# Eight placing transfers instead of twelve, and unit-first step order in the first eighth of every phase

## The chip, the cores and the metric

The kernel runs on one core of a Trainium2 chip. The metric is device time in microseconds (us). A core has five instruction streams that run side by side and meet through semaphores: TensorE (PE, with its weight loads PEld), VectorE (DVE), ScalarE (ACT), GpSimd (POOL) and SyncE (SP), which here only issues transfers (DMAs). Each stream is in order: an instruction that waits holds up all that stand behind it.

## The reference, cut to what matters

Four residual layers act on images `(4, 32, 32, 16)`. Three are of one kind, and they make up nearly all the work; layer 2 is another, small computation on intervals. For a layer of the first kind, with `n` the group-normalised input:

```python
first  = einsum('ijyx,byxc->bijc', M, n)
kern   = transpose(G, (0, 1, 5, 4, 2, 3)).reshape(h * w * f, c, 3, 3)
shifted = conv(n, kern, 'SAME')          # a 3x3 convolution with 1024*16 filters
diff   = relu(n[:, None, None] - shifted)
second = einsum('ijyx,bijyxc->bijc', W, diff)
x      = x + first - second
```

For each of the 1024 places (i, j), each filter f and each image b there is a whole 32x32 picture, which is clipped, weighted with `W` and summed to one number.

## The kernel before, in words

The four images go in two groups `g` of two (`GB` = 2). A phase is one group in one of the three convolution layers, six in all, in the order layer 0 group 0, layer 0 group 1, layer 1 group 0, and so on. The 1024 places are eight blocks `t` of 128 (`NT` = 8). In a block there are 32 steps, one for each filter f and image b. So a phase has 256 steps, and the program 1536. They are all issued by `conv_layer` (L707).

One step makes a 128x1024 picture in a pair of PSUM banks (there are four such pairs): `first_part` (L642) issues eight matmuls on `ib` and `ia`, ACT scales the pair in place (L663), and `second_part` (L666) adds six matmuls on `iyz` and `im9`. Then one DVE instruction (L680, tile `junk`) takes the minimum with zero, multiplies by the chunk of `W` (tile `WT`) and adds up. Step k's second part is issued after step k+1's first part.

The matmuls reach more than the precision of one pass by splitting both operands into a high and a low part. Weights: `prep_parts` (L220) makes, for each unit of four filters (`FU` = 4; 192 units, eight steps each), the tiles `parts` and `W9`. DVE cuts off the high part (L203, tile `upper_w`), ACT and POOL make the others (L236 to L245), POOL subtracts the centre tap from the next unit's raw weights (L214), and SP copies one half of `parts` to the other with halves swapped (L251) and loads raw weights two units ahead (L110). Its `yield`s spread these over the eight steps of a unit.

Images: before a phase, `before_conv` (L368) normalises the next group, writes it to DRAM, reads it back shifted (L392, tile `raw`), and then, for each of the two images b in turn:

- `split` (L274): DVE cuts the high part (L203, tile `upper_x`), POOL subtracts it (L280, twice, for the two slots s), and ACT scales it (L284, twice). The results are `tz` and `ty`, the two halves (index k) of one tile `temp`, laid out as (k, s, b, n) with n = 512. In the first phase the tile is `first`, and DVE takes POOL's place.
- `place` (L290): SP copies pieces of `ty` and `tz` into `ia` (L298) and `ib` (L300).
- `difference` (L286, L288): POOL (DVE in the first phase) writes `iyz`; then `halve_rest` (L178) on DVE finishes `im9`.

The generator `behind` (L733) hands these out a bit after each step, so their place in every engine's order is fixed when the program is built. For phases 1 to 3 the images are split and placed well inside the phase before; for phases 4 and 5, whose interval layer comes first, in the last eighth of it.

Each SP transfer uses one of eight completion semaphores in turn. So a transfer's issue waits until the transfer eight issues earlier has landed.

Before the change the 32 steps of a block run filter by filter, image 0 then image 1. Only in the very first block (`n == 0`) are they sorted by unit: four filters of image 0, then the same four of image 1.

Of the kernel before, what the change touches and what calls it, by code (L numbers as in the profile page):

```python
# [8 lines left out]
F32 = mybir.dt.float32  # L9
F32R = mybir.dt.float32r  # L10
# [5 lines left out]
P = 128  # L16
B, H, C = 4, 32, 16
NG = 2
GB = B // NG
# [5 lines left out]
HW = H // 2  # L25
WP = HW + 2
PITCH = H * WP
NH = H * HW
RUN = (H - 1) * WP + HW
LAST = (H - 1) * HW  # L30
TAPS = ((0, 1, 2, 3), (6, 7, 4, 5))
TEMP = 2 * 2 * GB * NH
# [12 lines left out]
def net_kernel(ctx: ExitStack, tc: tile.TileContext, x, xq, xi, convs, iv_w, iv_b, out):  # L45
# [26 lines left out]
    nc = tc.nc  # L72
# [6 lines left out]
    big = ctx.enter_context(tc.tile_pool(name="big", bufs=1))  # L79
# [32 lines left out]
    def load_chunk(n):  # L112
        if n < n_chunks:
            t = n % NT
            chunks[n] = wpool.tile([P, NP], F32, tag="WT", name=f"WT_{n}")
            nc.sync.dma_start(chunks[n], convs[phases[n // NT][1]][1][t * P : (t + 1) * P, :])
# [15 lines left out]
    first = big.tile([P, 8192], F32, tag="big", name="first")  # L132
    used = PLAIN * 3 * FU * P
# [40 lines left out]
    def halve(dst, src, mask):  # L174
        nc.scalar.activation(dst, src, AF.Copy, scale=mask[:, 1:2])  # L175

    def halve_rest(dst, src, mask):
        nc.vector.scalar_tensor_tensor(  # L178
            dst, src, mask[:, 0:1], dst.bitcast(F32), op0=ALU.mult, op1=ALU.add
        )  # L180
# [13 lines left out]
    QUARTERS = [(slice(64 * h, 64 * h + 32), slice(64 * h + 32, 64 * h + 64)) for h in range(2)]  # L194

    def image(v, x):
        return v.rearrange("... (y x) -> ... y x", x=x)[..., :HW]
# [69 lines left out]
    def prep_plain_rest(u, at=0, to=FU):  # L267
        halve_rest(units[u][3][:, at:to], raws[u][:, 2, at:to], low_p)

    def halves(temp, b):  # L270
        v = temp.rearrange("p (k s b n) -> p k s b n", k=2, s=2, b=GB)
        return v[:, 0, :, b], v[:, 1, :, b]

    def split(eng, g, b, temp, name, pause=IDLE):  # L274

        ty, tz = halves(temp, b)
        high = upper(image(raw[:, :2, b], WP), 2, f"x{name}{b}")
        yield 1
        for s in range(2):
            eng.tensor_tensor(  # L280
                image(tz[:, s], HW), image(raw[:, s, b], WP), image(high[:, s], HW), ALU.subtract
            )
            yield pause
            nc.scalar.activation(ty[:, s], high[:, s], AF.Copy, scale=EPS)  # L284

    def difference(eng, g, b, s, temp):  # L286
        ty, tz = (v.bitcast(F32)[:, s] for v in halves(temp, b))
        eng.tensor_tensor(iyz[g][:, s, b], ty, tz, ALU.subtract)  # L288

    def place(g, b, temp):  # L290

        ty, tz = (v.bitcast(F32) for v in halves(temp, b))
        da, db = (v[g].bitcast(F32)[:, :, b] for v in (ia, ib))
        for h, (lo, hi) in enumerate(QUARTERS):
            for s in range(2):
                at = HW if s == h else 0
                for to, src in ((lo, ty), (hi, tz)):
                    nc.sync.dma_start(da[to, s, :LAST], src[lo, s, at : at + LAST])  # L298
            for to, src in ((lo, ty), (hi, tz)):
                nc.sync.dma_start(db[to], src[hi])  # L300
        yield 1


# [64 lines left out]
    def before_conv(g, layer):  # L368
        xn = work.tile([P, NT, GC], F32, tag="xn", bufs=2, name=f"xn_{g}_{layer}")
        xns[g] = xn  # L370
        yield from group_norm(g, f"c{g}{layer}", xn, 1 if layer == 2 else 4)

        nc.vector.transpose(
            xt[g][:, :, 1 : 1 + H], xn
        )
        inner = xs[g][:, :, WP : WP + H * WP].rearrange("p h (t r n) -> p h r t n", r=ROWS, n=WP)
        for r in range(ROWS):
            for h in range(2):  # L380
                nc.sync.dma_start(
                    inner[:, h, r], xt[g][GC * r : GC * (r + 1), :, HW * h : HW * h + WP]
                )
        yield 2
        xsv = xs[g].rearrange("(b c) h n -> c h b n", b=GB)
        for slot, row, tap in [
            (slot, row, tap) for slot in range(2) for row, tap in enumerate(TAPS[slot])
        ] + [(2, row, 8) for row in range(4)]:
            for h in range(2):
                off = tap // 3 * WP + tap % 3  # L390
                r0 = 64 * h + C * row
                nc.sync.dma_start(  # L392
                    raw[r0 : r0 + C, slot ^ h if slot < 2 else 2, :, :RUN], xsv[:, h, :, off : off + RUN]
                )
            if layer < 2 or row % 2:
                yield 1
        yield 6 if layer == 2 else 12
        temp = big.tile([P, 8192], F32R, tag="big", name=f"temp_{g}{layer}")[:, :TEMP]
        for b in range(GB):
            yield from split(nc.gpsimd, g, b, temp, f"{g}{layer}")  # L400
            yield IDLE
            halve(image(im9[g][:, b], HW), image(raw[:, 2, b], WP), low_x)
            yield from place(g, b, temp)
            for s in range(2):
                difference(nc.gpsimd, g, b, s, temp)
            yield 1
            halve_rest(image(im9[g][:, b], HW), image(raw[:, 2, b], WP), low_x)
            yield 1
# [233 lines left out]
    def first_part(step):  # L642
        phase, t, f, b = step
        g = phases[phase][0]
        n = phase * NT + t
        u = n * NU + f // FU
        ps = bank_pair(f"pc_{n}_{f}_{b}")
        if u < PLAIN:
            products(
                ps,  # L650
                [(raws[u][:, s, f % FU], image(raw[:, s, b], WP)) for s in range(2)]
                + [(units[u][3][:, f % FU], im9[g][:, b])],
                True, {2: without_last},
            )
            return ps
        WU, WL, WD, W9 = (w[..., f % FU, :] for w in units[u])
        products(
            ps,
            [(WL[:, s], ib[g][:, s, b]) for s in range(2)]
            + [(WU[:, s], ia[g][:, s, b]) for s in range(2)],  # L660
            True, {2 + s: without_outer(s) for s in range(2)},
        )
        nc.scalar.activation(ps, ps, AF.Copy, scale=1.0 + EPS)  # L663
        return ps
# [42 lines left out]
    def conv_layer(phase, behind):  # L707


        kind, wait = 1, 0  # L710
        accs[phase] = work.tile([P, NT, GC], F32, tag="acc", bufs=2, name=f"acc_{phase}")
        for t in range(NT):
            n = phase * NT + t
            steps = [(f, b) for f in range(C) for b in range(GB)]
            if n == 0:
                steps.sort(key=lambda s: (s[0] // FU, s[1]))
            for at, (f, b) in enumerate(steps):
                may = next(parts, (IDLE, CALM)) if n or at >= FIRST else (IDLE, CALM)
                if n == 0 and at in (20, 24):
                    next(parts)  # L720
                if at == 4:
                    load_chunk(n + 1)
                step = (phase, t, f, b)
                open_steps.append((step, first_part(step)))
                if len(open_steps) > 1:
                    second_part(*open_steps.pop(0))
                wait -= 1
                if wait <= 0 and (kind > 0 or kind in may):
                    kind = wait = next(behind, 1 << 20)
        for _ in behind:  # L730
            pass
# [137 lines left out]
    def rest_of_start():  # L869

        nc.sync.dma_start(X[0], x[0])
        load_raw(2)
        load_raw(3)
        prep_plain_rest(0, F0, FU)
        for slot in (0, 1, 2):
            normal(nc.vector, 1, slot)
            sides(nc.vector, 1, slot)
        halve(image(im9[0][:, 1], HW), image(raw[:, 2, 1], WP), low_x)
        prep_plain(1)
        prep(2)  # L880
        yield 1
        halve_rest(image(im9[0][:, 1], HW), image(raw[:, 2, 1], WP), low_x)
        prep_plain_rest(1)
        yield 2
        temp = first.bitcast(F32R)[:, used : used + TEMP]
        for b in range(GB):
            yield from split(nc.vector, 0, b, temp, "00", 1)
            yield from place(0, b, temp)
            for s in range(2):
                difference(nc.vector, 0, b, s, temp)  # L890
            yield 1
        nc.gpsimd.memset(zero, 0.0)
        nc.vector.memset(part, 0.0)
        zeros(0)
        xns[0] = work.tile([P, NT, GC], F32, tag="xn", bufs=2, name="xn_00")
        yield from group_norm(0, "c00", xns[0], 4)

    parts = prep_parts()
# [81 lines left out]
```

## Time and profile before

| | us |
|---|---|
| median of three runs | 2477.86 (2477.18 to 2479.97) |
| the profiled execution | 2478.41 |
| its span, first to last instruction | 2476.7 |
| PE busy | 2458.2 |
| DVE / ACT / POOL busy | 2087.3 / 1878.4 / 1579.7 |
| L680 on DVE, mean of one | 1.224 |
| placing transfers: `ia` from `temp` x80, from `first` x16; `ib` x40 and x8 | to landing 3.4 and 2.6 (medians for `temp`) |
| raw weights (L110) x190 | to landing 7.1 |

In the rows of the profile, "out<-in" names what an instruction writes and reads, "Lnn" is the line of the program, and "<-" in a bracket names what ended the idle time before the instruction. "SPq" is SP's issue of a transfer. The granted clock of TensorE was 1.0 for the whole span.

### The profile page before, as it was taken

How to read it: one execution, taken by the hardware profiler on the slowest of the kernel's cores; microseconds unless marked ns; L12 is line 12 of the kernel's file. 1: busy time of each engine (PE TensorE's matmuls, PEld its weight loads, DVE VectorE, ACT ScalarE, POOL GpSimd, SP SyncE). 2: the span in 40 equal slices, each digit the busy share in tenths (PEclk: the TensorE clock that was granted, in tenths of full speed). 3: DMA queues.
4: the chain of work that ended last, by engine and by line, in shares of the span. 5: the costliest groups of instructions: out<-in, count | busy, mean ns of one | idle time of the engine just before them, and what ended most of it. 6: DMA issues, size and time to landing. Idle time of an engine off the chain costs nothing.

```text
span 2476.7 us, 58058 instructions
## 1 busy us (share of the span) xinstructions
PE 2458.2 (99%) x21906; PEld 2090.1 (84%) x21906; DVE 2087.3 (84%) x3617; ACT 1878.4 (76%) x2181; POOL 1579.7 (64%) x1750
## 2 busy tenths in 40 slices
PE   8999999999999999999999999999999999999999
PEld 5999888888888888888888988888998888888887
DVE  9888878888888888778898988899889888788887
ACT  4778767787777778777777777787777787677776
POOL 4766655666565657555567777586878676555552
PEclk9999999999999999999999999999999999999999
DMA  6446754466454467644454545574455467554442
GB/s 198 138 137 182 203 155 135 124 182 164 133 143 135 135 168 198 186 116 134 136 145 127 142 124 140 146 196 125 126 138 144 127 181 195 154 148 137 137 137 54
DMA packets 97673, 366.92 MB, mean 148 GB/s; under 512 B 26480, under 2 KB 31472, under 8 KB 97392
## 3 DMA queue, kind: packets, MB, share of 16 engines
q1 hardware_dynamic: 96832, 362.79, 53.0%
q8 instruction: 172, 2.82, 0.5%
q14 instruction: 109, 0.89, 0.1%
q10 hardware_dynamic: 432, 0.39, 0.1%
q0 software_dynamic: 128, 0.02, 0.0%
HBM read 199.78 MB, written 1.02 MB: 81 GB/s over the span
## 4 chain that ended last, share of the span: by engine, by line
PE 94%; DVE 2%; issue 1%; DMA 1%; ACT 0%; SPq 0%; POOL 0%; ACTq 0%; DVEq 0%; POOLq 0%
PE pc L627 93%; DVE junk L680 1%; PE pf L425 1%; DMA raw<-in_g 1%; ACT pc L663 0%; DMA first<-in_g 0%; SPq L298 0%; DVE raw L846 0%; SPq L300 0%; PE ps_l L548 0%; PE ps_r L561 0%; DMA parts<-parts 0%; DVE tables L508 0%; DVE raw L854 0%; DMA ib<-first 0%
## 5 line engine op out<-in xcount | busy, mean ns | idle before, releaser
L680 DVE SCALAR_TENSOR_TENSOR junk<-pc,WT 128x1024 f32<-128x1024 f32 x1536 | 1879.5, 1224 | 359.1 <-PE pc L627 308.3
L663 ACT ACTIVATE pc<-pc 128x1024 f32<-128x1024 f32 x1520 | 1532.0, 1008 | 561.0 <-PE pc L627 535.8
L627 PE MATMUL pc<-ib,parts 64*128 64x512 f32 x6080 | 958.5, 388 | 4.1 <-DVE junk L680 3.4
L627 PE MATMUL pc<-iyz,parts 64*128 64x512 f32 x6080 | 955.5, 387 | 2.2 <-ACT pc L663 2.0
L627 PE MATMUL pc<-ia,parts 64*128 64x496 f32 x6080 | 933.5, 379 | 0.0
L627 PEld LDWEIGHTS pc<-ia,parts 64*128 64x128 f32 x6080 | 595.5, 184 | 100.8
L627 PEld LDWEIGHTS pc<-ib,parts 64*128 64x128 f32 x6080 | 591.5, 184 | 105.0 <-DVE junk L680 9.9
L627 PEld LDWEIGHTS pc<-iyz,parts 64*128 64x128 f32 x6080 | 592.5, 184 | 88.4 <-ACT pc L663 6.4
L627 PE MATMUL pc<-im,W 64*128 64x496 f32 x3072 | 611.5, 384 | 0.0
L237 POOL TENSOR_TENSOR parts<-raw,upper_w 128x512 fp32r<-128x512 f32 x190 | 248.5, 1308 | 500.2 <-DVE upper_w L203 434.8
L627 PEld LDWEIGHTS pc<-im,W 64*128 64x128 f32 x3072 | 303.0, 184 | 54.5 <-issue 3.2
L243 POOL CAST parts<-parts 32x512 fp32r<-32x512 f32 x380 | 231.1, 608 | 50.1 <-ACT parts L240 31.8
L238 POOL TENSOR_TENSOR W<-W,raw 128x512 fp32r<-128x512 f32 x190 | 247.6, 1303 | 1.8 <-ACT W L175 1.8
L241 POOL TENSOR_TENSOR parts<-parts 128x512 fp32r<-128x512 f32 x190 | 246.8, 1299 | 2.0 <-ACT parts L236 1.9
L245 POOL CAST parts<-upper_w 32x512 fp32r<-32x512 f32 x380 | 231.6, 609 | 22.8
L214 POOL TENSOR_TENSOR raw<-raw,ident 128x512 f32<-128x512 f32 x190 | 199.9, 1052 | 52.2 <-DMA raw<-in_g 28.7
L175 ACT ACTIVATE W<-raw,low_w 128x512 fp32r<-128x512 f32 x190 | 136.2, 717 | 0.1
L680 DVE DVE_READ_ACCUMULATOR junk<-pc,WT 128x1 f32 x1536 | 127.5, 83 | 0.0
L236 ACT ACTIVATE parts<-upper_w 128x512 fp32r<-128x512 f32 x190 | 118.8, 625 | 6.6 <-DVE upper_w L203 6.4
L240 ACT CAST parts<-upper_w 128x512 fp32r<-128x512 f32 x190 | 116.5, 613 | 0.0
L695 POOL TENSOR_SCALAR acc<-acc 128x32 f32<-128x32 f32 x40 | 16.4, 409 | 141.7 <-DVE junk L680 139.7
L203 DVE TENSOR_SCALAR upper_w<-raw 128x512 int32<-128x512 int32 x190 | 86.1, 453 | 1.2 <-POOL raw L214 0.9
(139 smaller groups left out, 479.4 us busy)
## 6 DMA issues: line engine op xcount, KB each, us to landing
raw<-in_g SPq DMA_DIRECT2D x190, 768.0 KB, 7.1
parts<-parts SPq DMA_DIRECT2D x380, 384.0 KB, 4.9
WT<-in_w SPq DMA_DIRECT2D x48, 512.0 KB, 4.6
MT<-in_mt SPq DMA_DIRECT2D x24, 512.0 KB, 7.4
raw<-xs SPq DMA_DIRECT2D x120, 71.8 KB, 2.9
ib<-temp SPq DMA_DIRECT2D x40, 128.0 KB, 2.6
ia<-temp SPq DMA_DIRECT2D x80, 62.0 KB, 3.4
ib<-first SPq DMA_DIRECT2D x8, 128.0 KB, 2.4
```

The costliest lines, as they stand in the source:

```text
L175: nc.scalar.activation(dst, src, AF.Copy, scale=mask[:, 1:2])
L214: eng.tensor_tensor(raws[u][:, s, at:to], raws[u][:, s, at:to], pick[s][:, f0 + at : f0 + to].unsqueeze(2).to_broadcast([P, to - at, P]), ...
L236: nc.scalar.activation(WD, high, AF.Copy, scale=-EPS)
L237: nc.gpsimd.tensor_tensor(WL, w8, high, ALU.subtract)
L238: nc.gpsimd.tensor_tensor(W9, W9.bitcast(F32), src[:, 2], ALU.add)
L240: nc.scalar.copy(WU, high)
L241: nc.gpsimd.tensor_tensor(WD, WD.bitcast(F32), WL.bitcast(F32), ALU.add)
L243: nc.gpsimd.tensor_copy(WU[hi], WL[lo].bitcast(F32))
L245: nc.gpsimd.tensor_copy(WL[lo], high[hi])
L627: nc.tensor.matmul(ps[:, h, at : at + n], lhsT=w[r], rhs=v[r] if n == NH else v[r][:, :n], start=first and k == 0, stop=k == len(pairs) - ...
L663: nc.scalar.activation(ps, ps, AF.Copy, scale=1.0 + EPS)
L680: nc.vector.scalar_tensor_tensor(junk, ps.rearrange("p h n -> p (h n)"), 0.0, chunks[n], op0=ALU.min, op1=ALU.mult, accum_out=accs[phase][ ...
```

## The change

`place` issues eight transfers instead of twelve. The four `ib` copies (32 partitions x 2 x 512) come first. The eight `ia` copies (32 x 496, one for each slot s) become four of 32 x 2 x 496, which take both slots at once. The two slots are read from different offsets, so the source is a window of the whole tile with a pitch of 1008 or 1040 elements between its two rows. To reach that far, `temp` is no longer cut at `TEMP` = 4096 elements. The bytes moved are the same.

In `conv_layer`, the steps are sorted by unit in the first block of every phase (`t == 0`), not only in the first of all.

```diff
     def halves(temp, b):
-        v = temp.rearrange("p (k s b n) -> p k s b n", k=2, s=2, b=GB)
+        v = temp[:, :TEMP].rearrange("p (k s b n) -> p k s b n", k=2, s=2, b=GB)
         return v[:, 0, :, b], v[:, 1, :, b]
...
     def place(g, b, temp):
 
-        ty, tz = (v.bitcast(F32) for v in halves(temp, b))
+        parts = halves(temp.bitcast(F32)[:, :TEMP], b)
         da, db = (v[g].bitcast(F32)[:, :, b] for v in (ia, ib))
+        for lo, hi in QUARTERS:
+            for to, src in zip((lo, hi), parts):
+                nc.sync.dma_start(db[to], src[hi])
         for h, (lo, hi) in enumerate(QUARTERS):
-            for s in range(2):
-                at = HW if s == h else 0
-                for to, src in ((lo, ty), (hi, tz)):
-                    nc.sync.dma_start(da[to, s, :LAST], src[lo, s, at : at + LAST])
-            for to, src in ((lo, ty), (hi, tz)):
-                nc.sync.dma_start(db[to], src[hi])
+            for k, to in enumerate((lo, hi)):
+                at = (2 * k * GB + b) * NH + HW * (1 - h)
+                pitch = GB * NH + HW * (2 * h - 1)
+                src = temp.bitcast(F32)[lo, at : at + 2 * pitch].rearrange("p (s n) -> p s n", s=2)
+                nc.sync.dma_start(da[to, :, :LAST], src[:, :, :LAST])
         yield 1
...
-        temp = big.tile([P, 8192], F32R, tag="big", name=f"temp_{g}{layer}")[:, :TEMP]
+        temp = big.tile([P, 8192], F32R, tag="big", name=f"temp_{g}{layer}")
...
-            if n == 0:
+            if t == 0:
                 steps.sort(key=lambda s: (s[0] // FU, s[1]))
...
-        temp = first.bitcast(F32R)[:, used : used + TEMP]
+        temp = first.bitcast(F32R)[:, used:]
```

## The prediction

> **What bounds the kernel now.** I read the page's first and fourth parts, then PE's waits, then the timelines of SP, POOL and DVE around each place where images are placed.
>
> ```profile
> PE 2458.2 (99%) x21906; PEld 2090.1 (84%) x21906; DVE 2087.3 (84%) x3617; ACT 1878.4 (76%) x2181; POOL 1579.7 (64%) x1750
> ...
> PE 94%; DVE 2%; issue 1%; DMA 1%; ACT 0%; SPq 0%; POOL 0%; ACTq 0%; DVEq 0%; POOLq 0%
> ```
>
> ```profile
> engine line waited for: us in total, times, longest us
> PE ps_own L808 <- DVE s L806: 4.0, 1, 4.0
> PE pc L627 <- DVE junk L680: 3.4, 9, 0.5
> PE pc L627 <- DVE raw L846: 2.7, 1, 2.7
> PE pc L627 <- ACT pc L663: 2.0, 5, 0.4
> PE ps_v L800 <- DVE by_batch_v L799: 1.4, 1, 1.4
> PE pc L627 <- DMA ib<-first: 0.6, 1, 0.6
> ```
>
> PE is the bound. All its waits come to 14 us, some 8 of them before the first step. A real step takes 1.57 us of PE (the chain's longest PE piece: 3584 matmuls in 401.52 us, 14 a step). So there are 6 us to win after the start, and the change can win only the part that a placing transfer causes: the last row, 0.6. What it can lose is open: any new lateness that reaches PE.
>
> How much lateness PE takes is set by the four bank pairs: the first matmul of step k+4 needs the end of DVE's L680 of step k. In undisturbed steps PE arrives 1.65 us after that end (the trace's starts and ends). DVE gains only 0.2 us a step (1.57 against 1.37 for an L680 and what follows it), so after extra DVE work the lead stays short for several steps.
>
> **The change, part by part.**
>
> *Step order (phases 1 to 5, first eighth).* Matmuls, weights, reductions and the place of every other instruction stay; only which image is read differs. Both orders are in the trace: PE ran 0.112 us a matmul in the piece from 50.5 us, which begins in the sorted block, as in the later, unsorted ones. The second image is needed three steps (4.7 us) later, but nothing waited there: the last placing transfer for phase 4 landed at 1641 us and for phase 5 at 2055, both before their phases' first steps (1652 and 2063). Cost 0.
>
> *Twelve transfers to eight.* There are 12 calls, so 48 issues fewer at about 0.62 us each (median `ia` 0.59, `ib` 0.62): 30 us of SP, of which nearly all is covered, since PE never waits for SP but once. That once: at 49.9 us PE waits 0.62 us for the last `ib<-first`, which stands twelfth (issued 47.98, landed 50.38). Put among the first four it is issued near 39 us. It then lies in the ring behind the raw load, which landed at 45.45, so it lands by about 45. Gain **0.6**. After the first image's placing for phase 1 (231 to 238 us) L251 and L110 come about 2.4 us earlier; at 247 us POOL's L214 waits 0.37 us for that raw load, ahead of a DVE delay that PE feels (a 0.48 us gap at 253). Gain **0.3**.
>
> *A wait that is added.* In the changed program's instruction order, POOL's first L280 of the second image waits for two completion semaphores that it did not wait for before: those of the sixth and eighth transfers of the first image's `place`. Their source window now spans two rows, and the second image's row lies between them, so the program treats L280's write as an overlap. When would the eighth have landed? Phases 1 to 3: the transfers start at 230.7, 540.4 and 941.9 (after ACT's second L284), the eighth is issued about 4.4 us later and needs about 2.4 (`ib` alone), so it lands at 237.5, 547.2 and 948.7; POOL came to L280 at 239.04, 548.71 and 950.27. Covered by 1.5 us. In phase 0 DVE has this wait: landing about 34 against 34.91, covered, narrowly. For phases 4 and 5 it is not covered. SP and POOL before phase 4:
>
> ```profile
> 1616.44 0.53 SPq L110 DMA_DIRECT2D raw<-in_g  x1
> 1617.07 3.20 SPq L298 DMA_DIRECT2D ia<-temp  x4
> 1620.32 1.30 SPq L300 DMA_DIRECT2D ib<-temp  x2
> 1621.66 3.89 SPq L298 DMA_DIRECT2D ia<-temp  x4
> ```
>
> ```profile
> 1621.14 1.78 POOL L238 TENSOR_TENSOR W<-W,raw 128x512 fp32r<-128x512 f32 x1
> 1622.87 1.23 POOL L280 TENSOR_TENSOR temp<-raw,upper_x 128x512 fp32r<-128x512 f32 x1
> ...
> 1628.11 1.04 POOL L214 TENSOR_TENSOR raw<-raw,ident 128x512 f32<-128x512 f32 x1
> 1629.11 1.21 POOL L280 TENSOR_TENSOR temp<-raw,upper_x 128x512 fp32r<-128x512 f32 x1
> ```
>
> The raw load of 1616.44 landed 7.3 us later, at 1623.73. The eighth transfer after it uses its semaphore, so it is issued at 1623.75 (as the eighth was before), and seven others still lie in the ring. Before, seven of 580 kB in all landed by 1625.33, 1.6 us after the raw load, and the eighth 0.4 later. After, the seven have 905 kB: 2.5 us by proportion, 1626.2, and the eighth near 1626.6. L280 is then **3.75 us** late. Before phase 5 the raw load landed at 2035.24, the seven took 2.0 us, so 3.1, and the eighth is there near 2038.7 against L280 at 2034.38: **4.3 us**.
>
> What stands behind L280 on POOL is the weights' L241, L243, L245 and L214. Who waits: DVE's L203 of the next unit, for L214, and DVE's queue of L680s behind it:
>
> ```profile
> 1629.65 0.95 DVE L203 TENSOR_SCALAR upper_w<-raw 128x512 int32<-128x512 int32 x1
> 1630.52 1.21 DVE L680 SCALAR_TENSOR_TENSOR junk<-pc,WT 128x1024 f32<-128x1024 f32 x1
> ...
> 1631.66 1.89 DVE L178 SCALAR_TENSOR_TENSOR im<-raw,low_x,im 128x512 fp32r<-128x512 f32 x1
> 1633.48 1.21 DVE L680 SCALAR_TENSOR_TENSOR junk<-pc,WT 128x1024 f32<-128x1024 f32 x1
> ```
>
> L203 ended 0.28 us after the L280 beside it (1630.32). The same holds before phase 5 (2041.81 and 2042.09). So L203's end moves by all of POOL's lateness. The L680 that starts at 1633.48 already had PE waiting (0.53 us): PE moves by the whole **3.75**. Before phase 5 the least lead in the steps after L203 is 0.53, so PE moves by 4.3 - 0.5 = **3.8**. ACT's L236 also waits for L203, at the same time, so that is not added. The weights are not late as well: they had 5 to 6 us to spare, and their use moves with PE.
>
> **The skill.** *SBUF — State Buffer*, "SBUF: two separate sides": GpSimd and VectorE share one port pair as an exclusive lock, and the loser waits for the whole instruction. The trace agrees: L203 takes 0.42 us alone, 0.95 beside L280, and ends only after it. The forecast takes the rule, and its size from these rows. *DMA: Bandwidth & Descriptors*, "Queues, rings and completion order": an engine consumes descriptors in ring order. The trace agrees: the `ia` issued at 1617.07 landed at 1624.02, 0.29 us behind the raw load, though such a transfer alone takes 2.0. The forecast goes by the trace's sizes.
>
> **Sum.** 3.75 + 3.8 - 0.6 - 0.3 = +6.6 us. The profiled execution was 2478.41, 0.55 above the median, so 2485.0 for one like it, and 2477.86 + 6.6 = **2484.5** against the median. Bounds of the unknown landing: 2.3 us after its issue (an `ib` alone) makes both L280s 3.2 late, 3.2 + 2.7 - 0.9 = +5.0 (2482.9); 4.9 us after it (the 3.9 of the slowest `ia` that had no raw load ahead of it, and 1 more for the ring, a choice) makes both 5.8 late, 5.8 + 5.3 - 0.9 = +10.2 (2488.1).
>
> **Rivals.**
> - *DVE's lead takes it (not slower).* Were the full 1.65 us of lead there at L203, PE would move by 2.1 and 2.65: +3.9, 2481.7. It decides below +5.0 (0.2%; smaller differences a measurement of this kernel can't tell from none). Against it: PE's gap of 0.53 at 1634.22 shows the lead used up.
> - *The wait is over when POOL comes.* Then only the start gains: -0.9, 2477.0. It needs the eighth landed by 1622.9, before the raw load ahead of it. Against it: ring order.
> - *The new wait also bites in phases 0 to 3*, where 1.5 us (phase 0: less) cover it: if transfers of two rows need 3.9 instead of 2.4. That exceeds the cover by nothing to 0.5 us a phase: at most some 2 us more, 2486.5.
> - *Faster by over 0.2%* would need nearly all of PE's gaps to go: I see no way.
>
> **Chances.** Forecast 0.60 and the heavier case 0.08: slower, 0.68. DVE's lead 0.15 and no wait 0.13: within 0.2%, 0.28. Faster 0.04. The range 2478.5 to 2488.5 leaves out the no-wait case, the faster one and a small tail.
>
> **What would show it.** PE's gaps waiting for L680 near 1634 and 2046 us grow from 0.5 and 0 to about 4 each, or are split with waits for ACT's L663; POOL's L280 shows an idle of 3 to 4 us ended by `ia<-temp`; DVE's L203 waits for POOL's L214. PE's wait for `ib<-first` is gone. If POOL's L280 shows no such wait, or DVE's L203 comes no later, the prediction is wrong at that step; if PE slows between the placings, the step order was mis-costed.

## The result and the profile after

| | before | after |
|---|---|---|
| median, us (5 runs each) | 2477.86 (2476.06 to 2479.97) | 2489.31 (2487.78 to 2492.22) |
| the profiled execution, us | 2478.41 | 2488.05 |
| its span, us | 2476.7 | 2486.3 |
| all PE gaps of over 60 ns after its first matmul, us | 10.4 | 15.7 |

The ratio is 1.0045 (95% interval 1.0034 to 1.0056): slower by 11.5 us, against a forecast of +6.6. In experiments 1 to 4, before is the median of 33 executions, one of which took 5042.63 us and is left out of the ratios. Line numbers behind L290 have moved by a few: placing is now L296 (`ib`) and L302 (`ia`), the matmuls L629, ACT's scaling L665, and DVE's reduction L682.

The page of the kernel after: busy times, and the chain that ended last.

```profile
PE 2462.5 (99%) x21906; PEld 2068.9 (83%) x21906; DVE 2088.9 (84%) x3617; ACT 1878.5 (76%) x2181; POOL 1578.4 (63%) x1750
...
PE 94%; DVE 2%; DMA 1%; issue 1%; ACT 1%; POOL 0%; SPq 0%; ACTq 0%; DVEq 0%; POOLq 0%
```

DVE, ACT and POOL are busy within 1.6 us of what they were (PEld 21 us less, which was not followed up). PE is busy 4.3 us longer with the same 21906 matmuls. So the profile's +9.6 us is not only standing still (+5.3): PE was also slower at times.

PE's waits in the kernel after:

```profile
engine line waited for: us in total, times, longest us
PE pc L629 <- DVE junk L682: 9.2, 10, 3.5
PE ps_own L810 <- DVE s L808: 4.1, 1, 4.1
PE pc L629 <- DVE raw L848: 2.5, 1, 2.5
PE pc L629 <- ACT pc L665: 2.4, 6, 0.4
```

The wait for `ib<-first` is gone, and the waits for the reduction grew from 3.4 to 9.2 us. Where did this happen? I set each step's first matmul in the trace after against the same step before. After is ahead by 0.6 us at 253 us and by 0.7 at 966. It is level (0.04 ahead) at 1544, and 0.3 behind at 1628. Then it is **4.7 behind** at 1639, 4.3 at 2039, and **9.6 behind** from 2057 to the end. So the loss arises at the placings for phases 4 and 5, in two stretches of 11 and 18 us.

SP at the first of them (columns: start, duration, what, how many):

```profile
1616.60 0.54 SPq L110 DMA_DIRECT2D raw<-in_g  x1
1617.24 3.23 SPq L296 DMA_DIRECT2D ib<-temp  x4
1620.52 4.42 SPq L302 DMA_DIRECT2D ia<-temp  x4
```

The raw load landed at 1624.33 by the trace's landing times, and the eight transfers one after the other behind it, from 1624.67 to 1627.42. POOL there:

```profile
1627.58 1.22 POOL L280 TENSOR_TENSOR temp<-raw,upper_x 128x512 fp32r<-128x512 f32 x1 [4.41 <-DMA ia<-temp]
...
1632.81 1.04 POOL L214 TENSOR_TENSOR raw<-raw,ident 128x512 f32<-128x512 f32 x1
1633.80 1.20 POOL L280 TENSOR_TENSOR temp<-raw,upper_x 128x512 fp32r<-128x512 f32 x1
```

The added wait is there: L280 starts 0.16 us after the eighth transfer landed and 4.7 us later than before. L214 follows, 4.7 late too. DVE at that place:

```profile
1633.88 1.40 DVE L203 TENSOR_SCALAR upper_w<-raw 128x512 int32<-128x512 int32 x1 [3.90 <-POOL raw L214]
1635.21 1.21 DVE L682 SCALAR_TENSOR_TENSOR junk<-pc,WT 128x1024 f32<-128x1024 f32 x1
1636.35 1.85 DVE L178 SCALAR_TENSOR_TENSOR im<-raw,low_x,im 128x512 fp32r<-128x512 f32 x1
1638.12 1.21 DVE L682 SCALAR_TENSOR_TENSOR junk<-pc,WT 128x1024 f32<-128x1024 f32 x1
```

L203 ends at 1635.28, again 0.28 us after the L280 beside it. The two L682s stand 4.7 and 4.6 us later than the L680s of before. And PE:

```profile
1632.57 0.38 PE L629 MATMUL pc<-im,W 64*128 64x496 f32 x2
1636.48 1.22 PE L629 MATMUL pc<-ib,parts 64*128 64x512 f32 x4 [3.52 <-DVE junk L682]
1637.50 1.03 PE L629 MATMUL pc<-ia,parts 64*128 64x496 f32 x4
1638.33 1.05 PE L629 MATMUL pc<-iyz,parts 64*128 64x512 f32 x4
1639.18 0.45 PE L629 MATMUL pc<-im,W 64*128 64x496 f32 x2
1639.47 0.65 PE L629 MATMUL pc<-ib,parts 64*128 64x512 f32 x4
```

PE stands still for 3.52 us. Then four matmuls take 1.22 us where four of the same kind take 0.65 a step later. The trace's clock record has TensorE at **half speed** for 3.4 us from 1635.9, and again for 3.4 us from 2052.3, after the second standstill (3.08 us). I had not foreseen this. As a mean over 4 us it reads 0.58 and 0.57 (columns: window, its length, busy us and number of instructions of PE and PEld, DVE, ACT, POOL, then PE's clock, DMA share, GB/s):

```profile
1636.00:1640.00 4.00, 3.52 (x20) 2.66 (x22) 3.87 (x6) 2.40 (x3) 4.00 (x4) 0.58 0.96 226
...
2052.00:2056.00 4.00, 3.76 (x22) 2.57 (x20) 3.73 (x6) 1.49 (x2) 4.00 (x4) 0.57 0.93 217
```

Before the change the record has half speed only from 2475.6 us on, in the last 1.1 us of the span (so the 1.0 given above for the whole span holds but for that end).

Before phase 5, POOL's L280 and the two L288 that follow:

```profile
2042.67 1.22 POOL L280 TENSOR_TENSOR temp<-raw,upper_x 128x512 fp32r<-128x512 f32 x1 [5.69 <-ACT pc L665]
...
2050.05 2.70 POOL L288 TENSOR_TENSOR iyz<-temp 128x512 fp32r<-128x512 f32 x2
```

The bracket names an ACT instruction, but the eighth transfer landed at 2042.51, 0.16 us ahead, as in phase 4. It is the same wait under another name. DVE at the same place, after and then before:

```profile
2050.29 1.21 DVE L682 SCALAR_TENSOR_TENSOR junk<-pc,WT 128x1024 f32<-128x1024 f32 x1
2051.43 1.86 DVE L178 SCALAR_TENSOR_TENSOR im<-raw,low_x,im 128x512 fp32r<-128x512 f32 x1
2053.22 1.21 DVE L682 SCALAR_TENSOR_TENSOR junk<-pc,WT 128x1024 f32<-128x1024 f32 x1
```

```profile
2042.01 1.21 DVE L680 SCALAR_TENSOR_TENSOR junk<-pc,WT 128x1024 f32<-128x1024 f32 x1
2043.15 0.74 DVE L178 SCALAR_TENSOR_TENSOR im<-raw,low_x,im 128x512 fp32r<-128x512 f32 x1
2043.82 1.21 DVE L680 SCALAR_TENSOR_TENSOR junk<-pc,WT 128x1024 f32<-128x1024 f32 x1
```

L178 takes 1.12 us more. In both kernels POOL's two L288 run beside it. Before, POOL was the one held up (3.29 us for its two). After, POOL takes 2.70, and DVE's L178 ends 0.54 us after the second of them. PE there:

```profile
2051.56 0.73 PE L629 MATMUL pc<-ib,parts 64*128 64x512 f32 x4 [3.08 <-DVE junk L682]
...
2054.49 1.22 PE L629 MATMUL pc<-ib,parts 64*128 64x512 f32 x4 [0.24 <-DVE junk L682]
```

It was a near tie. One by one, L178 and the second L288 began at 2043.15 and 2043.21 before, and at 2051.43 and 2051.46 after. In the six kernels up to experiment 4 there are 39 such pairs; L178 is recorded as the first in 35, by at most 0.06 us, and was the one held up in 24 of these. So the starts do not tell who is held up. At this one place, ahead of phase 5, it was DVE in the three kernels in which L280 waits (after, experiments 1 and 4) and POOL in the three in which it does not (before, experiments 2 and 3).

### The profile page after: what moved, and what is told of

Read it like the earlier page. It is cut to its first block, busy times and chain, and to the rows that moved or that the text cites. A ratio compares the mean times of both kernels' runs of the same rounds, so it can differ in the third digit from the quotient of the medians.

```text
span 2486.3 us, 57989 instructions
## 1 busy us (share of the span) xinstructions
PE 2462.5 (99%) x21906; PEld 2068.9 (83%) x21906; DVE 2088.9 (84%) x3617; ACT 1878.5 (76%) x2181; POOL 1578.4 (63%) x1750
## 4 chain that ended last, share of the span: by engine, by line
PE 94%; DVE 2%; DMA 1%; issue 1%; ACT 1%; POOL 0%; SPq 0%; ACTq 0%; DVEq 0%; POOLq 0%
PE pc L629 93%; DVE junk L682 1%; DMA raw<-in_g 1%; PE pf L427 1%; ACT pc L665 0%; DMA first<-in_g 0%; SPq L394 0%; PE ps_l L550 0%; PE ps_r L563 0%; SPq L383 0%; DVE tables L510 0%; DMA ia<-temp 0%; POOL parts L241 0%; POOL parts L245 0%; POOL parts L243 0%
## 5 line engine op out<-in xcount | busy, mean ns | idle before, releaser
L682 DVE SCALAR_TENSOR_TENSOR junk<-pc,WT 128x1024 f32<-128x1024 f32 x1536 | 1879.6, 1224 | 360.4 <-PE pc L629 310.0
L665 ACT ACTIVATE pc<-pc 128x1024 f32<-128x1024 f32 x1520 | 1531.9, 1008 | 562.6 <-PE pc L629 537.6
L629 PE MATMUL pc<-ib,parts 64*128 64x512 f32 x6080 | 955.4, 388 | 9.3 <-DVE junk L682 9.2
L629 PE MATMUL pc<-iyz,parts 64*128 64x512 f32 x6080 | 952.8, 387 | 2.5 <-ACT pc L665 2.4
L629 PE MATMUL pc<-ia,parts 64*128 64x496 f32 x6080 | 930.5, 380 | 0.0
L629 PEld LDWEIGHTS pc<-ib,parts 64*128 64x128 f32 x6080 | 584.9, 185 | 117.3 <-DVE junk L682 16.6
L629 PEld LDWEIGHTS pc<-ia,parts 64*128 64x128 f32 x6080 | 588.8, 185 | 107.9
L629 PEld LDWEIGHTS pc<-iyz,parts 64*128 64x128 f32 x6080 | 586.5, 185 | 95.4 <-ACT pc L665 7.3
L629 PE MATMUL pc<-im,W 64*128 64x496 f32 x3072 | 608.1, 384 | 0.0
L629 PEld LDWEIGHTS pc<-im,W 64*128 64x128 f32 x3072 | 299.4, 185 | 58.2 <-issue 3.5
L214 POOL TENSOR_TENSOR raw<-raw,ident 128x512 f32<-128x512 f32 x190 | 199.5, 1050 | 46.3 <-DMA raw<-in_g 19.9
L682 DVE DVE_READ_ACCUMULATOR junk<-pc,WT 128x1 f32 x1536 | 127.5, 83 | 0.0
L203 DVE TENSOR_SCALAR upper_w<-raw 128x512 int32<-128x512 int32 x190 | 86.9, 458 | 8.3 <-POOL raw L214 7.9
```

The costliest lines, as they stand in the source:

```text
L214: eng.tensor_tensor(raws[u][:, s, at:to], raws[u][:, s, at:to], pick[s][:, f0 + at : f0 + to].unsqueeze(2).to_broadcast([P, to - at, P]), ...
L629: nc.tensor.matmul(ps[:, h, at : at + n], lhsT=w[r], rhs=v[r] if n == NH else v[r][:, :n], start=first and k == 0, stop=k == len(pairs) - ...
L682: nc.vector.scalar_tensor_tensor(junk, ps.rearrange("p h n -> p (h n)"), 0.0, chunks[n], op0=ALU.min, op1=ALU.mult, accum_out=accs[phase][ ...
```

## The experiments

**1. The new placing with the old order.** My theory puts the whole loss in the placing; the rival is that the sorted order of the first eighth costs something.

```diff
-            if t == 0:
+            if n == 0:
```

> The changed placing with the old step order (only the very first block unit-first). If the wait that POOL's L280 now has is the whole loss: as slow as the changed kernel, near 2489, with L280 again 4 to 5 us late at the end of phases 3 and 4 and PE gaps of 3 to 3.5 us there. If the step order carries part of the loss: nearer to 2478 by that part.

Measured 2488.09 (2486.92 to 2490.06), ratio 1.0037 (1.0024 to 1.0051). The placing alone makes the loss. In its profile PE stands still for 3.6 and 5.3 us at the two places (I had expected 3 to 3.5), with half clock for 3.4 and 6.8 us behind them.

**2. The new order with the old placing.** The kernel before with one line changed.

```diff
-            if n == 0:
+            if t == 0:
```

> The old twelve transfers with the new step order. If the order costs nothing: 2477.9, within 0.1% of before, with the same PE gaps. If it costs or gains: up to several us either way, in the first 50 us of each phase.

Measured 2478.74 against 2478.64 for before, ratio 1.0002 (0.9994 to 1.0010). The order costs nothing that can be measured.

**3. Eight transfers, without the overlap.** The kernel after, with `temp` laid out image by image, so that the window of an image's transfer spans no row of the other image. Transfers, bytes, sizes and order are the same.

```diff
-        v = temp[:, :TEMP].rearrange("p (k s b n) -> p k s b n", k=2, s=2, b=GB)
-        return v[:, 0, :, b], v[:, 1, :, b]
+        v = temp[:, :TEMP].rearrange("p (b k s n) -> p b k s n", k=2, s=2, b=GB)
+        return v[:, b, 0], v[:, b, 1]
...
-                at = (2 * k * GB + b) * NH + HW * (1 - h)
-                pitch = GB * NH + HW * (2 * h - 1)
+                at = (2 * b + k) * 2 * NH + HW * (1 - h)
+                pitch = NH + HW * (2 * h - 1)
```

> The whole change, but temp laid out as (image, k, s, n) in place of (k, s, image, n), so that each image's source window lies in its own 2048 elements and nothing of the other image stands between its two rows. The transfers keep their number, order and bytes. If the wait is the whole loss: L280 of the second image no longer waits for transfers, and the time is before's less 0.6 to 1, near 2477. If eight wider transfers, their order or the step order cost by themselves: near 2489, or in between.

Measured 2478.18, ratio 0.9996 (0.9988 to 1.0005). The loss is gone, while the transfers are nearly as slow as in the kernel after (medians to landing 6.1 us for `ib` and 4.9 for `ia`; after 6.8 and 5.2, before 2.6 and 3.4). So the late landing does no harm by itself: the wait does. POOL's second-image L280 for phase 4, and PE's next stop, in this kernel:

```profile
1620.84 1.22 POOL L280 TENSOR_TENSOR temp<-raw,upper_x 128x512 fp32r<-128x512 f32 x1
```

```profile
1632.73 0.73 PE L629 MATMUL pc<-ib,parts 64*128 64x512 f32 x4 [0.49 <-DVE junk L682]
```

L280 starts with no wait, although the eighth transfer landed only at 1625.29, 4.4 us later, and PE's stop is what it was before the change (0.53). That also says what eight transfers are worth in place of twelve: this profile ends 1.4 us ahead of before, but the medians don't tell the two apart.

**4. The wait made shorter.** The kernel after, with the two `ia` transfers for which L280 waits issued first instead of sixth and eighth.

```diff
-        for lo, hi in QUARTERS:
-            for to, src in zip((lo, hi), parts):
-                nc.sync.dma_start(db[to], src[hi])
-        for h, (lo, hi) in enumerate(QUARTERS):
-            for k, to in enumerate((lo, hi)):
+        for k in (1, 0):
+            for h, (lo, hi) in enumerate(QUARTERS):
+                to = (lo, hi)[k]
...
+        for lo, hi in QUARTERS:
+            for to, src in zip((lo, hi), parts):
+                nc.sync.dma_start(db[to], src[hi])
```

> The whole change with the two transfers that L280 waits for issued first and second instead of sixth and eighth. The wait stays. In the changed kernel the second of the eight landed 2.1 us (phase 4) and 2.6 us (phase 5) ahead of the eighth. If the loss follows the landing of those two: L280 about 2 us late instead of 4.4, PE gaps of 1 to 1.5 us, no stretch at half clock, and +4 us, near 2482. If the loss does not hang on that landing: near 2489.

Measured 2481.92 (2479.93 to 2482.74), ratio 1.0012 (1.0004 to 1.0021): the size of the loss follows the length of the wait. POOL and PE at phase 4 in this kernel (the bracket at L280 names ACT, but the second transfer landed at 1623.56, 0.16 us ahead of it, as in the kernel after):

```profile
1623.72 1.22 POOL L280 TENSOR_TENSOR temp<-raw,upper_x 128x512 fp32r<-128x512 f32 x1 [2.36 <-ACT pc L666]
```

```profile
1632.63 0.74 PE L630 MATMUL pc<-ib,parts 64*128 64x512 f32 x4 [1.52 <-DVE junk L683]
1633.21 0.62 PE L630 MATMUL pc<-ia,parts 64*128 64x496 f32 x4
...
1635.57 0.73 PE L630 MATMUL pc<-ib,parts 64*128 64x512 f32 x4 [1.05 <-DVE junk L683]
1636.14 0.61 PE L630 MATMUL pc<-ia,parts 64*128 64x496 f32 x4
```

The lateness reaches PE in two stops, one for each of the two late reductions, and neither brings half clock. In the kernel after, the second stop is not seen: the half clock fills it.

**5. Standstills by themselves.** What does half clock cost, and what brings it? The kernel before, with DVE kept busy by n extra reductions of 1.22 us at step 12 of eleven blocks (n is 2 to 8, by a table `DELAYS` that isn't printed here).

```diff
+    extra = const.tile([P, 1], F32, name="extra")
...
+                if at == 12:
+                    for _ in range(DELAYS.get((phase, t), 0)):
+                        nc.vector.tensor_reduce(extra, chunks[n], axis=AX.X, op=ALU.add)
```

> The kernel before with extra work put in DVE's order at the thirteenth step of eleven blocks that are otherwise quiet: 2 to 8 reductions of a 128x1024 tile, of some 1.15 us each. The result is unchanged. By DVE's lead of 1.65 us PE should stand still for about 0.6 (2), 1.8 (3), 2.9 (4), 4.1 (5), 5.2 (6), 6.4 (7) and 7.5 us (8). If a standstill of PE of about 3 us is what brings the granted clock to half for 3.4 us: such a stretch after each gap of 3 us or more and after none below, 6 to 8 of them, and 2520 to 2531 us. If the half clock in the changed kernel had another cause: no such stretches, or not behind the gaps, and about 2521.

Measured 2593.35 (ratio 1.0457), 113 us more: the size was missed by far. The standstills were as meant: one of 3.2 us and all of 3.8 or more brought half clock, one of 3.26 did not. But the steps between them took 1.606 us in place of 1.567 (median). I suspected the tile `extra`, which moves later tiles by four bytes, and took it apart in the next three.

**6. The same without a new tile.** The reductions write into a column of `squares`; 3, 4 or 5 of them.

> The kernel before, with VectorE kept busy by 3, 4 or 5 extra reductions of 1.22 us at step 12 of eleven units (two threes, six fours, three fives), their results written into a column of `squares`, so that no tile moves. It measures the price of a standstill of TensorE by itself. If TensorE's clock goes to half after a standstill of about 3 us or more: gaps near 1.9 (threes), 3.2 (fours) and 3.9 us (fives); no half-clock stretch after the threes, a stretch of 3.4 us after each of the fives and after some of the fours; each stretch costs about 1.7 us on top of its gap. In all some 35 us of gaps and 5 to 15 us of slow running: 2519 to 2529 us. If the half clock in the changed kernel comes from something else in it (its transfers, say), no stretch appears here and the time is near 2513. Steps elsewhere stay at 1.567 us.

Measured 2531.68 (ratio 1.0219, 1.019 to 1.0249), 53.9 us more, 2.7 above the range I had expected; quiet steps took 1.567 us. PE's gaps grew by 36.3 us. Half clock came after nine of the eleven delays, 37.5 us of it in all, more than I expected (two stretches were 6.8 long, and one came after a "three"). The rest, 53.9 - 36.3 = 17.6 us, makes 0.47 us lost for each us of half clock: **1.6 us for a stretch of 3.4**. (PE stood still for 3.4 of the 37.5; half clock costs nothing then. For each us in which PE worked it is about 0.5.)

All changes of the clock in this trace lie on one grid of 3.4133 us: the first four stretches of half clock begin at 245.30, 357.94, 566.15 and 774.37, which is 33, 61 and 61 intervals apart. Here are two standstills of 2.72 us each, at 667.16 and at 1197.60, with the grid's intervals as windows (columns as above):

```profile
665.14:668.55 3.41, 2.02 (x20) 1.34 (x16) 3.34 (x3) 1.84 (x2) 2.00 (x3) 1.00 0.41 86
668.55:671.96 3.41, 2.08 (x18) 1.75 (x20) 3.14 (x6) 0.85 (x1) 0.00 (x0) 1.00 0.92 216
671.96:675.37 3.41, 3.41 (x34) 2.85 (x32) 3.14 (x7) 2.27 (x4) 0.00 (x0) 1.00 0.41 163
1197.62:1201.03 3.41, 0.72 (x6) 0.63 (x8) 3.24 (x5) 0.35 (x1) 0.09 (x1) 1.00 0.98 231
1201.03:1204.44 3.41, 3.41 (x20) 2.70 (x18) 3.06 (x6) 1.01 (x1) 0.00 (x0) 0.50 0.74 235
```

The first lies across two intervals, PE is busy for 2.0 us in each, and the clock stays at 1.00. The second lies in one, PE is busy for 0.7 us in it, and the next interval runs at 0.50: 20 matmuls instead of 34.

**7 and 8. Only a tile.** The kernel before with one unused tile ahead of the others, of 4 bytes a partition, then of 64. No instruction is added.

```diff
+    const.tile([P, 1], F32, name="extra")
```

> The kernel before, with one unused tile of four bytes a partition laid ahead of the others, so that all later addresses in SBUF move by four bytes; no instruction is added. If that move alone is what made each step 1.606 us in place of 1.566 in the run with the delays up to 8, the time is near 2478 + 1520 x 0.04 = 2540 us. If the slower steps came from the added reductions, it stays at 2478.

> The kernel before, with the unused tile made 64 bytes a partition in place of four; no instruction is added. If what slows the steps is the low bits of the addresses (matmul operands no longer on a boundary of 64 bytes), this move keeps them and the time is back near 2478. If any other layout than the one before is slower, as with four bytes (2530.85), it is near 2530.

Measured 2530.85 (ratio 1.0216, 1.0186 to 1.0246) and 2540.54 (ratio 1.0246, 1.0217 to 1.0276). The median step is 1.567 us before, 1.607 with 4 bytes and 1.613 with 64. The extra time is spread: at a step near 700 us each of the seven pairs of matmuls took 3 to 8 ns more with 4 bytes. The 113 us of experiment 5 part as follows. With the 4-byte tile alone PE is busy 56.2 us longer than before. In experiment 5 it is busy 70.9 longer, and its gaps grow by 42.4. The remaining 14.7 us of busy time go with 41.0 us of half clock, during 13 of which PE stood still, so again about 0.5 for each us in which it worked. The low six bits of the addresses alone are not the cause, since 64 bytes, which keep them, do as much harm. What about the layout matters stays open.

## Why the prediction failed, point by point

The sign and the path of the added wait held (L280, L214, L203, L680, PE). The gain at the start did not last, two costs behind the wait were put at nothing, and the time fell 0.8 us above the range. The profiled execution itself (2488.05) lies inside it, but partly by luck: the room up to 2488.5 was made for a landing 4.9 us after the eighth issue, and it took 3.1 and 3.3. In the trace's own sum:

| term, us | forecast | measured in the profile |
|---|---|---|
| start, and after the placing for phase 1 | -0.9 | 0 (-0.7 at 966, 0 at 1544) |
| phase 4: L280 late, and PE moved by | 3.75, 3.75 | 4.4, 4.4 |
| phase 5: L280 late | 4.3 | 4.0 |
| phase 5: DVE's lead takes | -0.5 | -0.5 |
| phase 5: L178 held up | 0 | +1.1 |
| phase 5: half clock | 0 | +0.7 |
| phase 5: PE moved by | 3.8 | 5.3 |
| sum | +6.6 | +9.7 |

(Each measured lateness is L280's start after minus before, less what PE was already behind: 1627.58 - 1622.87 - 0.3, and 2042.67 - 2034.38 - 4.3. The 0.3 that PE was behind at 1628 and the 0.4 that it made good between the placings nearly cancel; in the trace it ends 9.6 behind.) Of the 3 us between forecast and trace, 0.9 is the gain that did not last, 0.6 the landing before phase 4, and 1.5 what happened before phase 5.

- **Step order, cost 0.** Right: no cost that can be measured (experiments 2 and 1).
- **"Gain 0.6" and "Gain 0.3".** The waits named did go, and PE was 0.6 to 0.7 ahead until 966 us. The step that failed is that this would last. At 51 us PE was 0.9 ahead, and then waited 0.42 at 52.19 for ACT's scaling. The rest went at 1543, where eight small matmuls of the interval layer (L550) began 0.7 us earlier and ended when they did before. They take 1.44 us instead of 0.75. That is not the placing's doing alone: in experiment 2, with the old placing, they take 1.46, and in experiment 3, with the new placing and order, 0.81. Why stays open.
- **The added wait.** Right in place and kind: L280, not covered before phases 4 and 5 and covered before 1 to 3 (eighth landed 238.54, 547.54, 949.03; L280 at 238.76, 548.10, 950.02). The cover was thinner than the 1.5 us of the forecast, 0.2 us at the first, because the eighth transfer needed 3.3 us there in place of 2.4. In phase 0 it was not covered: DVE's L280 came at 35.13 behind a landing at 35.01, which costs at most the 0.2 by which it came later. So the rival of a wait in phases 0 to 3 fell, though by little.
- **"PE moves by the whole 3.75."** PE did move by the whole lateness in phase 4. What was mis-sized is the landing. The forecast took seven transfers by proportion to their bytes, 2.5 us behind the raw load; they took 2.8 (1624.33 to 1627.12). The raw load itself landed 0.6 us later than before. The ring order on which this rested, from the Trainium skill's *DMA: Bandwidth & Descriptors*, "Queues, rings and completion order", agrees with the trace: the eight landed in the order of their issue (1624.67 to 1627.42).
- **"Before phase 5 the least lead is 0.53, so PE moves by 3.8."** This step failed. It took L178 at its old 0.74 us. With POOL and DVE shifted together, which of the two waits for the other at L178 and L288 came out the other way, and L178 took 1.86. The exclusive lock that I cited for L203 (the Trainium skill's *SBUF — State Buffer*, "SBUF: two separate sides") takes in VectorE instructions with two inputs in SBUF beside a GpSimd instruction that reads SBUF, so L178 beside L288 too; I applied it to one pair and not to the next. That DVE would lose here could not be read off the trace before (a near tie, 0.06 us apart); that it might could, at a price of up to 1.1 us.
- **TensorE at full clock throughout.** Taken for granted without a word, and wrong. It cost only what later waits did not cover. In phase 4 that was next to nothing: the step after it (1639.47) still started only 0.14 us after the late reduction that ended at 1639.33, and its floor is 0.06. In phase 5 PE fell 0.7 us further behind after its last wait for DVE (8.9 at 2054, 9.6 at 2057). In experiment 1, with 6.8 us of half clock, it fell 1.3 further there (10.3 to 11.6).
- **The other 1.8 us.** The median lies 11.45 above that of before, the profile only 9.6. The five executions order themselves by mean granted clock: 2487.8 and 2488.1 us at 0.999, 2489.3 and 2490.4 at 0.998, 2492.2 at 0.997. More half clock in the slower ones fits this, and so does experiment 1's profile (2490.1 at 0.998, with 10.2 us of half clock), but of the five only the one of 2488.05 has a trace. It is argued, not shown.
- **DVE's lead takes it; the wait is over when POOL comes; faster.** The first two fell by PE's 4.4 and L280's 4.41 of idle. For the last, experiment 3 shows that even without the wait the gain can't be measured.

No version tried beats the kernel before by a measurable amount. In PE's standing still not much is left: its gaps were 10.4 us there, 4.2 of them ahead of the first step. Whether some other layout makes a step shorter than 1.567 us was not tried.

## What to carry to other kernels

Merging strided pieces into one transfer widens the stretch that its source is taken to span: look at which later writes now count as overlapping it, and lay the data out so that they don't (experiment 3), or issue the transfers that are waited for first (experiment 4). When a lateness is carried forward through two engines that share a port, ask at every pair of instructions that run side by side who will wait, not only at the first pair. On an engine that is the bound, price a standstill of over 2 us with the slower clock that can follow it (the shortest that brought it here was 2.46 us), unless later waits hide that.

## What the runs showed of the hardware

- **TensorE's clock follows its standstills on a fixed grid.** In all ten traces, set against a grid of 3.413 us and leaving out the program's first 20 us and its end, an interval at full clock with PE idle for 1.96 us or more was followed by one at half clock (20 cases), and one with 1.74 or less never was. After a half-clock interval, the clock was back when PE had been idle for 0.57 us or less in it, and was not at 0.74 or more. So a standstill of 2.46 us brought half clock (experiment 6, at 242.9), and one of 3.26, cut by the grid into 1.51 and 1.74, passed without (experiment 5, at 567.4). The Trainium skill's *TensorE: Matmul & The Clock Gate*, "Part 1: The HAM clock gate (the "warmup" mystery)", has a free-running window of 3413 ns, and half rate after an idle one. The traces agree on the length, and on free running in that the grid lies at different offsets from the program's start (first change at 14.58 us in the kernel after, 12.08 in experiment 3, 13.20 in experiment 6); here a window need not be idle throughout, some 57% of it was enough.
- **Four bytes can cost 2%.** An unused tile of 4 bytes a partition made the median step 1.607 us instead of 1.567. An experiment that adds a tile must show that quiet steps keep their time, or it measures the layout as well.
